# A selective-scan network: pairs of images with 128 channels on the partitions, changed to one image with 64 channels times two states and the other stages streamed beside the scans

## The chip, the cores and the metric

One core of one Trainium2 chip. The metric is the device time of one execution, in microseconds (us); the kernel before takes 12205 us. Engines: PE is TensorE (PEld its weight loads), DVE is VectorE, ACT is ScalarE, POOL is GpSimd, SP issues DMAs. PSUM is the memory that PE's products land in. The text takes each engine's instructions as carried out in their compiled order; in the changed kernel's trace VectorE's 7546 are.

## The reference, cut to what matters

Four images of 56x56 pixels and 96 channels pass four layers. Two of them hold a selective scan over 3136 positions, in four directions, with 192 channels and 16 states each:

```python
dt  = softplus(einsum(dt_raw, dtw) + dtb)          # dt_raw, b, c: projections of seq
d_a = exp(dt[..., None] * -exp(A_log))             # 192 x 16 per position
d_b = dt[..., None] * b[:, :, None, :]
def step(h, inp):
    da_t, db_t, x_t, c_t = inp
    h = da_t * h + db_t * x_t[..., None]           # the scan
    return h, einsum('bds,bs->bd', h, c_t)         # sum over the 16 states
y = ys + seq * D
# around it: layer norms, gates, 3x3 convolutions, a feed-forward;
# layers 2 and 3: linear attention and an fp8-quantized feed-forward
```

## The kernel before

A pair of images is loaded and passes all stages, one stage after the other. In the scan, 128 partitions hold 128 channels (a third tile holds the last 64 channels of both images). There are 3072 units (a chunk of 784 positions, a tile, a state). In each, ScalarE computes `da`; PE spreads the row of B over the partitions, into PSUM; VectorE multiplies it by `du` = dt times u and runs the scan; GpSimd multiplies the result `hs` by C, which gives `hc`; and PE adds `hc` up over the states:

```python
self.psum = ctx.enter_context(tc.tile_pool(name="psum", bufs=4, space=...PSUM))   # 4 tiles of 2 banks, for all uses
...
        yp = self.ps()                               # sums over the states of this slot
        def add_up(n, hc):
            for h in range(2):
                nc.tensor.matmul(yp[:, h, :HC], self.ident, hc[:, h * HC : (h + 1) * HC],
                                 start=n == 0, stop=n == NS - 1)
        ...
        for n in range(NS):
            ...
            nc.scalar.activation(da, dt, AF.Exp, scale=self.negA[l][:, t // 2, k, n : n + 1])
            db = b_of                                # PSUM: B spread over the partitions by PE
            nc.vector.tensor_tensor(db, du, db, ALU.mult)
            if n < NS - 1:
                b_of = spread_b(n + 1)
            if hc is not None:
                add_up(n - 1, hc)
            nc.vector.tensor_tensor_scan(hs[:, way], da[:, way], db[:, way], ..., ALU.mult, ALU.add)
            ...
            nc.gpsimd.tensor_tensor(hc, hs, cb, ALU.mult)    # times C
```

Of the four PSUM tiles one holds the sums, so three are free for spreads of B and the projections. (Cuts are marked by dots; the comments in code cuts are mine.)

## Time and profile before

| | before |
|---|---|
| time, median of its runs | 12205 us |
| four scans (windows of the prediction) | 9979 us |
| VectorE busy in a scan | 87% |
| all other stages | 2228 us |
| mean granted PE clock | 0.915 |

The prediction below shows and reads the lines. One line that it does not show matters later, the granted PE clock in 40 equal slices of the span, in tenths of full speed:

```profile
PEclk9999999899999989899989999998999999888999
```

### The profile page before, as it was taken

How to read it: one execution, taken by the hardware profiler on the slowest of the kernel's cores; microseconds unless marked ns; L12 is line 12 of the kernel's file. 1: busy time of each engine (PE TensorE's matmuls, PEld its weight loads, DVE VectorE, ACT ScalarE, POOL GpSimd, SP SyncE). 2: the span in 40 equal slices, each digit the busy share in tenths (PEclk: the TensorE clock that was granted, in tenths of full speed). 3: DMA queues.
4: the chain of work that ended last, by engine and by line, in shares of the span. 5: the costliest groups of instructions: out<-in, count | busy, mean ns of one | idle time of the engine just before them, and what ended most of it. 6: DMA issues, size and time to landing. Idle time of an engine off the chain costs nothing. (4 is left out here: it accounts for less than half of the span.)

```text
span 12206.9 us, 96092 instructions
## 1 busy us (share of the span) xinstructions
PE 9365.6 (77%) x32080; PEld 4295.8 (35%) x32080; DVE 9606.5 (79%) x7881; ACT 4411.3 (36%) x4763; POOL 6200.5 (51%) x5541
## 2 busy tenths in 40 slices
PE   6777777779777777779977777777787777777798
PEld 3333333334333333334533333333343333333345
DVE  6888888862888888893668888888638888888936
ACT  4333333332333333332343333333323333333323
POOL 3666566630666665660036666656316666656600
PEclk9999999899999989899989999998999999888999
DMA  4444434331444443440034443444214444333400
GB/s 126 125 128 126 122 120 127 119 93 49 128 126 128 124 122 120 122 124 24 4 122 127 128 126 121 122 122 124 88 55 127 126 128 125 119 120 120 124 24 9
DMA packets 279497, 1316.86 MB, mean 108 GB/s; under 512 B 61980, under 2 KB 72972, under 8 KB 278008
## 3 DMA queue, kind: packets, MB, share of 16 engines
q1 hardware_dynamic: 278080, 1307.13, 35.2%
q8 instruction: 252, 4.13, 0.1%
q10 hardware_dynamic: 920, 3.60, 0.1%
q14 instruction: 245, 2.01, 0.1%
HBM read 1270.44 MB, written 40.14 MB: 107 GB/s over the span
## 5 line engine op out<-in xcount | busy, mean ns | idle before, releaser
L552 PE MATMUL ps<-hc,ident 128*128 128x392 f32 x12288 | 5280.7, 560 | 2002.4 <-POOL hc L592 1998.1
L592 POOL TENSOR_TENSOR hc<-hs,X 128x784 f32<-128x784 f32 x3072 | 5667.8, 1850 | 864.6 <-DVE hs L586 522.7
L578 ACT ACTIVATE da<-dt,negA 128x784 f32<-128x784 f32 x3072 | 2913.0, 949 | 5786.7 <-DVE hs L586 5786.6
L586 DVE TENSOR_TENSOR_SCAN hs<-da,carry,ps 128x784 f32<-128x784 f32 x2304 | 4130.8, 1830 | 6.4
L552 PEld LDWEIGHTS ps<-hc,ident 128*128 128x128 f32 x12288 | 2316.0, 207 | 4579.2 <-POOL hc L592 3398.1
L580 DVE TENSOR_TENSOR ps<-du,ps 128x784 f32<-128x784 f32 x3072 | 2828.9, 963 | 560.2 <-PE ps L563 496.7
L590 POOL COPY carry<-hs 128x1 f32<-128x1 f32 x2304 | 474.9, 206 | 2240.8 <-DVE hs L586 2182.2
L586 DVE TENSOR_TENSOR_SCAN hs<-da,ps 128x784 f32<-128x784 f32 x768 | 1330.8, 1770 | 4.0 <-POOL hc L592 0.8
L501 POOL TENSOR_TENSOR bc<-rest,bc 32x784 bf16<-32x784 f32 x128 | 212.6, 1661 | 1871.0 <-ACT bc L500 1871.0
L560 PE MATMUL ps<-bc,sel 96*128 96x512 bf16 (+1 forms) x4096 | 936.2, 336 | 153.2 <-DVE hs L586 150.1
L563 PE MATMUL ps<-bc,sel 96*64 96x512 bf16 (+1 forms) x4096 | 546.8, 384 | 205.0 <-DVE hs L586 203.5
L560 PEld LDWEIGHTS <-sel 96*128 96x128 bf16 x4096 | 385.2, 99 | 819.5 <-issue 383.7
L532 DVE TENSOR_TENSOR du<-dt,U 128x784 f32<-128x784 f32 x192 | 345.7, 1800 | 364.3 <-ACT dt L527 364.3
L511 PE MATMUL ps<-dtr,dtw 12*128 12x392 f32 (+1 forms) x512 | 267.8, 654 | 238.4 <-ACT dtr L498 238.4
L563 PEld LDWEIGHTS <-sel 96*64 96x64 bf16 x4096 | 204.7, 121 | 668.5 <-DVE hs L586 316.8
L496 DVE TENSOR_TENSOR rest<-ps,bc 96x784 f32<-96x784 f32 x128 | 123.9, 968 | 390.9 <-ACT bc L495 373.3
L482 PE MATMUL ps<-U,w 128*108 128x392 f32 (+1 forms) x512 | 316.3, 704 | 0.0
L486 PE MATMUL ps<-U,w 128*108 128x392 f32 (+1 forms) x512 | 313.1, 697 | 0.0
L666 PE MATMUL ps<-Y,diag 128*128 128x392 f32 x864 | 289.0, 496 | 3.8 <-DVE diag L690 3.8
L527 ACT ACTIVATE dt<-ps,c 128x784 f32<-128x784 f32 x192 | 175.1, 914 | 233.4 <-PE ps L511 126.1
L511 PEld LDWEIGHTS ps<-dtr,dtw 12*128 12x128 f32 (+1 forms) x512 | 106.2, 229 | 369.1 <-ACT dtr L498 298.1
L361 PE MATMUL ps<-ln_r,spread 128*96 128x112 f32 x1792 | 212.9, 276 | 21.9 <-DVE ln_r L356 20.4
(177 smaller groups left out, 5459.8 us busy)
## 6 DMA issues: line engine op xcount, KB each, us to landing
X<-c SPq DMA_DIRECT2D x1024, 784.0 KB, 4.1
X<-c SPq DMA_DIRECT2D x1024, 392.0 KB, 5.2
z<-zs SPq DMA_DIRECT2D x48, 392.0 KB, 2.3
zl<-z SPq DMA_DIRECT2D x28, 672.0 KB, 4.5
x<-X SPq DMA_DIRECT2D x4, 2352.0 KB, 10.5
X<-x SPq DMA_DIRECT2D x4, 2352.0 KB, 13.7
c<-cf SPq DMA_DIRECT2D x128, 49.0 KB, 1.7
xin<-in_x_dram SPq DMA_DIRECT2D x4, 1176.0 KB, 8.8
```

The costliest lines, as they stand in the source:

```text
L482: nc.tensor.matmul(o, self.par("w128", f"{l}xw{k}a"), self.in_order(self.u3[:, j], orient, lo, HC), start=True, stop=False,)
L486: nc.tensor.matmul(o, self.par("w128", f"{l}xw{k}{j}"), self.in_order(self.u3[:, 2], orient, lo, HC), start=False, stop=True,)
L511: nc.tensor.matmul(ps[:, h, :HC], lhsT, rhs[t][:, h], start=True, stop=True)
L532: self.nc.vector.tensor_tensor(du.rearrange("p (a b) -> p a b", b=HS), dt.rearrange("p (a b) -> p a b", b=HS), self.in_order(self.u3[:, t] ...
L552: nc.tensor.matmul(yp[:, h, :HC], self.ident, hc[:, h * HC : (h + 1) * HC], start=n == 0, stop=n == NS - 1)
L560: nc.tensor.matmul(ps[:, s], self.sel[:, n, :], flat(bc[t])[:, s], start=True, stop=True)
L563: nc.tensor.matmul(ps[64 * j : 64 * j + 64, s], self.sel[:, n, :64], flat(bc[j])[:, s], start=True, stop=True,)
L578: nc.scalar.activation(da, dt, AF.Exp, scale=self.negA[l][:, t // 2, k, n : n + 1])
L580: nc.vector.tensor_tensor(db, du, db, ALU.mult)
L586: nc.vector.tensor_tensor_scan(hs[:, way], da[:, way], db[:, way], carry[:, t, n : n + 1] if step else 0.0, ALU.mult, ALU.add)
L590: nc.gpsimd.tensor_copy(carry[:, t, n : n + 1], hs[:, last : last + 1])
L592: nc.gpsimd.tensor_tensor(hc, hs, cb, ALU.mult)
```

## The change

Its intent: the scans are bound by VectorE and the other stages by PE, so let the stages of one image run while another image is scanned. One image at a time; 64 channels times two states on the partitions; what goes between stages passes through DRAM; the sums over states become pairs of products with 64 output columns; VectorE is relieved of some work. The diff has some 1700 lines; its core:

```diff
-        self.psum = ctx.enter_context(tc.tile_pool(name="psum", bufs=4, space=bass.MemoryType.PSUM))
+    def ps(self):                                   # everything else: 3 single banks
+        return self.psum.tile([128, 512], F32, tag="ps", name="ps", bufs=3)
+    def spread_b(self, ch, q):                      # B: 2 tiles of 2 banks
+        ps = self.psum.tile([128, 1024], F32, tag="b", name="b", bufs=2)
...
+        units = [(ch, g, q) for ch in chunks for g in range(NG) for q in range(NQ)]
...
+            nc.vector.tensor_tensor(db, ch.du[g], db, ALU.mult)
+            if n + 1 < len(units):
+                b = self.spread_b(units[n + 1][0], units[n + 1][2])
+            if late is not None:
+                self.add_up(*late)                  # sum of the unit before
+            nc.vector.tensor_tensor_scan(hs[:, way], da[:, way], db[:, way], ..., ALU.mult, ALU.add)
+            nc.scalar.copy(at, hs[:, end : end + 1])          # carry, was on GpSimd
+            nc.gpsimd.tensor_tensor(hc, hs, ch.cc[q // 2][:, q % 2], ALU.mult)
...
+        for h in range(2):                          # add_up: two states, 64 channels
+            nc.tensor.matmul(self.y[64 * h : 64 * h + 64, :HC], self.two,     # 128 x 64
+                             hc[:, h * HC : (h + 1) * HC], start=q == 0, stop=False)
...
+    for n, ch in enumerate(net.scans()):            # 8 phases: 2 layers x 4 images
+        ...
+            due = lengths[min(p, 7)] * u // (UNITS - NG * NQ)
+            while taken < due and next(rest, rest) is not rest:   # a step of another stage
+                taken += 1
+    for _ in net.tail(3):                           # the last image's tail, with nothing beside
+        pass
```

## The prediction

> **What bounds the kernel now.** I read the page's engine shares first, then the slices, then a table of windows cut where the scans begin and end, then the costliest groups, the waits of VectorE inside a scan, and one line by itself. (L... are lines of the kernel before.)
>
> ```profile
> PE 9365.6 (77%) x32080; PEld 4295.8 (35%) x32080; DVE 9606.5 (79%) x7881; ACT 4411.3 (36%) x4763; POOL 6200.5 (51%) x5541
> DVE  6888888862888888893668888888638888888936
> POOL 3666566630666665660036666656316666656600
> ```
>
> No engine is full over the span, but the slices show four long plateaus of VectorE at 8 or 9 tenths and between them holes where GpSimd falls to 0. The windows (columns: window, length, busy of PE, PEld, DVE, ACT, POOL, clock, DMA) give the sizes:
>
> ```profile
> 0.00:139.00 139.00, 90.18 (x482) 49.14 (x482) 55.41 (x89) 66.79 (x74) 8.30 (x20) 0.89 0.38 120
> 139.00:2641.00 2502.00, 1861.99 (x5594) 805.41 (x5594) 2184.85 (x1703) 920.31 (x988) 1542.43 (x1371) 0.91 0.41 124
> 2641.00:3027.00 386.00, 341.04 (x1334) 182.92 (x1333) 105.95 (x117) 111.67 (x118) 9.78 (x12) 0.95 0.12 39
> ...
> 5516.00:6234.00 718.00, 625.51 (x3514) 360.42 (x3512) 334.56 (x399) 252.51 (x286) 5.88 (x4) 0.93 0.10 29
> ...
> 11609.00:12207.00 598.00, 536.24 (x3033) 309.82 (x3032) 287.22 (x355) 189.70 (x220) 0.00 (x0) 0.95 0.05 13
> ```
>
> Four scans (two pairs of images, two layers) take 2502, 2489, 2499 and 2489 us, together 9979. The rest, 139 + 386 + 718 + 387 + 598 = 2228 us, is norms, convolutions, attention and feed-forward, bound by PE (536 of 598) while VectorE is under half busy. In a scan VectorE is busy 2185 of 2502 (87%), ScalarE 37%, GpSimd 62%. Which instructions these are:
>
> ```profile
> L592 POOL TENSOR_TENSOR hc<-hs,X 128x784 f32<-128x784 f32 x3072 | 5667.8, 1850 | 864.6 <-DVE hs L586 522.7
> L586 DVE TENSOR_TENSOR_SCAN hs<-da,carry,ps 128x784 f32<-128x784 f32 x2304 | 4130.8, 1830 | 6.4
> L580 DVE TENSOR_TENSOR ps<-du,ps 128x784 f32<-128x784 f32 x3072 | 2828.9, 963 | 560.2 <-PE ps L563 496.7
> L586 DVE TENSOR_TENSOR_SCAN hs<-da,ps 128x784 f32<-128x784 f32 x768 | 1330.8, 1770 | 4.0 <-POOL hc L592 0.8
> L532 DVE TENSOR_TENSOR du<-dt,U 128x784 f32<-128x784 f32 x192 | 345.7, 1800 | 364.3 <-ACT dt L527 364.3
> L602 DVE SCALAR_TENSOR_TENSOR Y<-ps,wts,Y 128x392 f32<-128x392 f32 x192 | 141.5, 781 | 46.2 <-PE ps L552 46.2
> L496 DVE TENSOR_TENSOR rest<-ps,bc 96x784 f32<-96x784 f32 x128 | 123.9, 968 | 390.9 <-ACT bc L495 373.3
> ```
>
> The 3072 pairs of a multiply and a scan cost 4130.8 + 1330.8 + 2828.9 = 8290.5 us of VectorE, with almost no idle before a scan. The idle of the scans, 4 x some 310 us, stands in front of du, rest and the first multiply behind them (364 + 391 + 560 us): the projections of the next chunk are made in VectorE's way, 64 times some 20 us.
>
> **What the Trainium skill says.** "SBUF — State Buffer", section "SBUF: two separate sides": a VectorE instruction with two SBUF inputs, or in a two-port mode, and a GpSimd instruction that reads SBUF exclude each other for a whole instruction. The trace agrees:
>
> ```profile
> L532 DVE TENSOR_TENSOR du<-dt,U x192: 949/1722/3003, 118.5 to 11533.6; 128x784 f32<-128x784 f32 x192
> L580 DVE TENSOR_TENSOR ps<-du,ps x3072: 944/964/989, 125.9 to 11594.8; 128x784 f32<-128x784 f32 x192
> ```
>
> The same size with one PSUM input never leaves 944 to 989 ns; with two SBUF inputs it goes from 949 to 3003. "ScalarE: Activation LUTs", section "What ACT_TABLE_LOAD costs": 1283 ns and a drain of 1380 ns. The loads of this trace take 1283 ns; in ScalarE's timeline the next instruction starts 0.01 us after one, so I see no drain and count 1283. "TensorEngine Tiling (Array Packing)", section "Available Configurations": an array of 128 rows by 64 columns is two tiles, which work independently. The trace has such pairs:
>
> ```profile
> L511 PE MATMUL ps<-dtr,dtw 12*128 12x392 f32 x256 | 135.1, 659 | 121.9 <-ACT dtr L498 121.9
> L514 PE MATMUL ps<-dtr,dtw 12*64 12x392 f32 x256 | 89.2, 845 | 0.0
> ```
>
> 128 columns occupy PE 135.1/256 = 0.53 us each, 64 columns 89.2/256 = 0.35, though one lasts longer: they overlap. (An fp32 matmul is two instructions in the trace.)
>
> **The change part by part.** *The scan core keeps its size.* The partitions hold 64 channels times two states in place of 128 channels, so 8 phases x 4 directions x 4 chunks x 3 groups x 8 state pairs = 3072 multiplies and scans of 128x784, as before, same operands: 8290 us. Nothing of that is gained.
>
> *VectorE loses* du (345.7, to GpSimd) and the sums into Y (141.5 + 130.0, now a matmul with the identity and a ScalarE copy). rest stays: 256 halves, some 133 us. *It gains beside the scans* what was in the holes. By my count of the compiled instructions at widths of 448: three loads, 21 x 0.62 = 13 us; four middles, six operations a chunk, 28 x 3.7 = 104; three tails, 21 x 13.2 = 277 (six in fusion, two in each gram, some eleven in each feed-forward). Together 394. Of these about 413 have two SBUF inputs or a fast fp16 form, and each can meet a GpSimd instruction of 1.85 us; from du (mean 1.80 against an undisturbed mean near 1.30) I put 0.7 us each: 290. Sum in the scans 8290 + 133 + 394 + 290 = 9107 us.
>
> *GpSimd:* hc 5668, du doubled (each half of the partitions needs it) 384 x 1.85 = 710, bc 213, small powers and memsets near 100; carry (475) leaves. 6700 us, not a bound by itself.
>
> *ScalarE:* da 2913; 2304 carries at an estimated 0.2 = 460; 768 softplus halves at 0.6 = 460; 768 copies of y at 0.5 = 385; projections' copies near 600; the rest of the net some 650; and 1051 table loads, where the page had some 140, because Exp alternates with Softplus, Silu and Gelu: 1051 x 1.283 = 1350. Sum 6800 us.
>
> *PE:* the sums over states become pairs of 64 columns, half of 5281 at best, so 2700 to 3500; spreading B near 1400; the other products 3500 to 4000. Some 8000. DMA falls: C is fetched once per chunk for all three groups, 1024 x 0.4 MB = 411 MB in place of most of 1307 MB.
>
> *Idle in the scans.* The next chunk is prepared a third of a chunk ahead, which should remove most of the 1240 us. But only two PSUM buffers are left for B, and on PE the spread for unit n+2 stands behind the sum of unit n-1, which waits for hc. The compiled order has 1141 places with two multiplies in a row. After scans ending at -1.8 and 0, hc ends at about 0.05, the sum near 0.9, the spread near 1.4, where the second multiply wanted it at 0.96: 0.45 us for perhaps half of them, 250 us. Each of 512 du and bc on GpSimd pushes hc by 1.7 to 1.85 us; say a third shows, 300. 224 chains of a norm (PE, ScalarE, power on GpSimd, PE, VectorE), beside the scans fewer, 0.5 each, 100; reloading U for 8 images, 60; other waits 100. These do not simply add, because a stall lets the others catch up; I take 650.
>
> *What is exposed.* Before the first scan: constants, folding, one image, near 130. After the last: the tail of one image. The tail of two took 598, bound by PE; one has less PE work (near 220 us by its matmuls) but only two chunks in flight and long chains: 340.
>
> Sum: 9107 + 650 + 130 + 340 = **10230 us** predicted, 16% under 12205.
>
> **The rivals.** *GpSimd and PE hold the scan through the buffers* (two of B, hs and hc each): if every insertion cost its full 1.85 us and every pair its 0.45, idle would be near 1450, some 11000 us. For it: everything runs in order, and hc ends just when it is wanted; against: GpSimd has 1 us spare in each unit. *ScalarE starves VectorE of da:* a table load out and back with a softplus is 3.2 us, gelu more, with da only three deep (5.6 us of scans). 6800 of 10000 speaks against a bound, bursts for it; 10600. *VectorE is simply full:* idle of 2%, shorter tail; 9107 + 180 + 450 gives 9740. *The stages beside do not fit* or their queues stall as the projections do today: 9979 for the scans as now, plus 394 + 290, less 617 moved away, plus 470, gives 10500. None reaches 12205; for that hiding would have to win nothing of 2228.
>
> **Range and chances.** From VectorE full (9740) to the buffers holding it in half of the cases (10700): 9750 to 10700. Faster by over 2% means under 11961: 0.96; within 2% 0.025; slower 0.015.
>
> **What would show it.** Right: multiplies and scans 3072 each near 960 and 1830 ns; VectorE at 91 to 95% in the scans; no holes in GpSimd's row until the end; tail(3) near 340 us; DMA bytes under half; sums on PE near 0.25 us busy per instruction. Wrong: multiplies that wait for PE in thousands of small gaps (buffers), scans that wait for ScalarE (tables), two-input operations far over 1.3 us, or a tail over 500 us. If GpSimd's hc grows beyond 1.85 us, the unit itself was misjudged.

## The result, and the profile after

The changed kernel takes 12851 us (median; 12819 to 12870 in 4 runs), against 12205 in the same rounds: ratio 1.052 (95% interval 1.050 to 1.055), **5% slower** where 16% faster was foretold. All ratios in this text are the mean time of one kernel's runs over that of the other's of the same rounds, so they are not quite the ratio of the medians quoted.

The first part of the page of the changed kernel, and two of its slices' rows:

```profile
PE 10724.2 (83%) x32510; PEld 3416.3 (27%) x32510; DVE 9010.8 (70%) x7546; ACT 6582.8 (51%) x10422; POOL 6985.7 (54%) x3964
DVE  4776777667776777767776666877668776777722
PEclk6766667766667667776767677766777667776665
```

The holes between the scans are gone, as intended, but VectorE is at 6 or 7 tenths where it was 8 or 9. And the row of the clock is the surprise: 6 and 7 tenths nearly everywhere, a mean of 0.689 in place of 0.915. Windows, cut at the first and the last scan (length, busy of PE, PEld, DVE, ACT, POOL, clock, DMA):

```profile
147.00:12274.00 12127.00, 10192.21 (x30858) 3118.33 (x30858) 8887.00 (x7246) 6441.77 (x10142) 6908.60 (x3865) 0.69 0.21 52
12274.00:12868.00 594.00, 442.34 (x1387) 246.75 (x1386) 102.12 (x221) 95.80 (x205) 50.84 (x57) 0.59 0.10 30
```

VectorE's 8887 us in the scans are close to the foretold 9107. Its idle there is 12127 - 8887 = 3240 us, and 650 were foretold. The costliest groups that answer to those of before (count, busy, mean ns, idle before and what ended most of it):

```profile
L537 POOL TENSOR_TENSOR hc<-hs,cc 128x784 f32<-128x784 f32 x3072 | 5704.9, 1870 | 4545.8 <-DVE hs L531 3550.0
L551 PE MATMUL y<-hc,two 128*64 128x392 f32 x12288 | 4120.3, 740 | 1294.4 <-POOL hc L537 1219.0
L524 DVE TENSOR_TENSOR b<-du,b 128x784 f32<-128x784 f32 x3072 | 2963.4, 970 | 2481.5 <-PE b L483 2468.6
L531 DVE TENSOR_TENSOR_SCAN hs<-da,carry,b 128x784 f32<-128x784 f32 x2304 | 4166.1, 1834 | 149.4 <-ACT da L522 91.7
```

The multiply and the scan take what they took (970 and 1834 ns), so does GpSimd's product. But in front of the multiply VectorE now waits 2469 us for PE's spread of B, in 1474 gaps. ScalarE, with its table loads, makes its scans wait only 113 us. The sums on PE (L551) occupy 4120/12288 = 0.335 us each, where the prediction hoped for 0.25 and half of the former 0.43 would be 0.215. How the clock shows in single instructions, from the timeline of the changed kernel (start, us, what):

```profile
3001.47 1.67 PE L455 MATMUL ps<-dtr,wd 12*128 12x392 f32 x2
...
3010.09 0.92 PE L455 MATMUL ps<-dtr,wd 12*128 12x392 f32 x2
```

The same two instructions take 1.67 us at one place and 0.92 at another; the clock's own records in the trace give 0.5 for the first place and 1.0 for the second. They know just these two values; the half lasts 8014 us in all in the changed kernel and 2083 in the one before. The two largest waits of PE (us in total, times, longest) are short ones:

```profile
PE y L551 <- POOL hc L537: 1219.0, 1240, 2.6
PE b L483 <- DVE hs L531: 486.3, 469, 3.7
```

Two counts that no view prints, made from the instructions in the traces, matter below. First, call a multiply that follows another multiply on VectorE, with no scan between, a *double*; the order is fixed when the kernel is compiled. The changed kernel has 1056 doubles (the prediction counted 1141). VectorE stands 1284 us in front of doubles and 1191 us in front of all other multiplies. Second, while VectorE stood there, 2475 us in all, PE was idle for only 40: it worked at spreads for 892 us, at sums for 552, at projections and the finishing of `y` for 503, and at other stages for 489. So VectorE waits for a PE that is busy with what stands in front of the spread.

### The profile page after: what moved, and what is told of

Same layout as the page of the kernel before. It is cut to its first block, busy times and chain, and to the rows that moved or that the text cites. A ratio compares the mean times of both kernels' runs of the same rounds, so it can differ in the third digit from the quotient of the medians. Undisturbed runs are those within 1.5% of the kernel's fastest.

```text
span 12868.3 us, 101763 instructions
## 1 busy us (share of the span) xinstructions
PE 10724.2 (83%) x32510; PEld 3416.3 (27%) x32510; DVE 9010.8 (70%) x7546; ACT 6582.8 (51%) x10422; POOL 6985.7 (54%) x3964
## 5 line engine op out<-in xcount | busy, mean ns | idle before, releaser
L537 POOL TENSOR_TENSOR hc<-hs,cc 128x784 f32<-128x784 f32 x3072 | 5704.9, 1870 | 4545.8 <-DVE hs L531 3550.0
L551 PE MATMUL y<-hc,two 128*64 128x392 f32 x12288 | 4120.3, 740 | 1294.4 <-POOL hc L537 1219.0
L524 DVE TENSOR_TENSOR b<-du,b 128x784 f32<-128x784 f32 x3072 | 2963.4, 970 | 2481.5 <-PE b L483 2468.6
L531 DVE TENSOR_TENSOR_SCAN hs<-da,carry,b 128x784 f32<-128x784 f32 x2304 | 4166.1, 1834 | 149.4 <-ACT da L522 91.7
L522 ACT ACTIVATE da<-dt,na 128x784 f32<-128x784 f32 x3072 | 2862.0, 945 | 728.9 <-DVE hs L531 714.1
L483 PE MATMUL b<-bc,sel 96*128 96x512 bf16 (+1 forms) x6144 | 2110.7, 436 | 489.9 <-DVE hs L531 486.3
L551 PEld LDWEIGHTS y<-hc,two 128*64 128x64 f32 x12288 | 839.8, 178 | 3117.3 <-POOL hc L537 2320.1
L531 DVE TENSOR_TENSOR_SCAN hs<-da,b 128x784 f32<-128x784 f32 x768 | 1346.3, 1774 | 54.4 <-ACT da L522 21.5
L431 PE MATMUL ps<-U,wd 64*108 64x392 f32 (+1 forms) x1536 | 864.0, 774 | 0.0
L461 POOL TENSOR_TENSOR du<-dt,U 128x784 f32<-128x784 f32 x384 | 783.0, 2047 | 147.0 <-ACT dt L456 138.9
L593 POOL TENSOR_TENSOR rs<-rs,power 112x4 f32<-112x4 f32 x252 | 257.4, 1021 | 964.6 <-ACT rs L592 784.8
L522 ACT ACT_TABLE_LOAD x511 | 655.6, 1283 | 8.3
L456 ACT ACT_TABLE_LOAD x339 | 434.9, 1283 | 78.9 <-PE ps L455 73.7
```

Source lines behind the costliest of these rows:

```text
L431: nc.tensor.matmul(ps[:m, :HC].rearrange("p (a b) -> p a b", b=HS), self.wx[rows, g, :m], self.in_order(self.U[rows, g], orient, c * CS + ...
L456: nc.scalar.activation(dt[:, h * HC : (h + 1) * HC], ps[:, :HC], AF.Softplus, bias=dtb[:, g : g + 1])
L461: nc.gpsimd.tensor_tensor(du.rearrange("p (a b) -> p a b", b=HS), ch.dt[g].rearrange("p (a b) -> p a b", b=HS), self.in_order(self.U[:, g] ...
L483: self.nc.tensor.matmul(ps[:, s], w, ch.bc[:, s], start=True, stop=True)
L522: nc.scalar.activation(da, ch.dt[g], AF.Exp, scale=ch.na[:, g, q : q + 1])
L524: nc.vector.tensor_tensor(db, ch.du[g], db, ALU.mult)
```

## The experiments

**Theory A (clock).** The paired 64-column sums use the array half as long; the granted clock then falls to a half for most of the time, each spread comes late, and VectorE waits for it. **Theory B (buffers and order).** With two tiles for B where the kernel before had three free, and the spread standing on PE behind a sum that waits for GpSimd, VectorE must wait whatever the clock. **Theory C.** The stages beside get in the way. Fifteen kernels ran. The five with the stages after the scans (sections 6 and 7) have a single run; I use them only for differences of some per cent between their phases. (A phase is the 384 units of one image and layer.)

### 1. Give PE its work back

```diff
+        nc.vector.tensor_scalar_mul(self.two, self.two, 0.5)
-        for h in range(2):
-            nc.tensor.matmul(..., self.two, hc[...], start=q == 0, stop=False)
+        for again in range(2):
+            for h in range(2):
+                nc.tensor.matmul(..., self.two, hc[...], start=q == 0 and again == 0, stop=False)
```

> The changed kernel with every sum over states issued twice at half weight (result unchanged), so PE has the array work per unit that the kernel before had. Theory A (the paired 64-column sums leave PE so idle that its clock is granted at half for 62% of the time, and the slow spread of B is what VectorE waits for): the clock rises from 0.689 to over 0.85, the first multiply's waits for the spread fall from 2469 us to under 1700, and the time falls below 12400 us although PE has more to do. Theory B (PE's order and two buffers of B, the clock being a by-product): more PE work in front of each spread makes the waits longer, over 3000 us, and the time over 13300 us.

12174 us, ratio to before 0.9975 (0.996 to 0.999): **5.3% less than the changed kernel by doing its sums twice.** The scans' window, the sums and VectorE's first wait in this run:

```profile
147.00:11581.00 11434.00, 10152.54 (x43136) 3587.33 (x43136) 8964.11 (x7245) 6399.95 (x10076) 6889.16 (x3864) 0.93 0.22 55
```

```profile
L553 PE MATMUL y<-hc,two 128*64 128x392 f32 x24576 | 5400.7, 542 | 997.3 <-POOL hc L538 911.0 <-issue 71.4 <-POOL du L462 1.0
```

```profile
DVE b L525 <- PE b L484: 1586.2, 957, 11.4
```

PE is busy for the same 10150 us with some 12,280 more matmul instructions: the clock is 0.93 in the scans in place of 0.69, and a matmul of the sums occupies PE 5401/24576 = 0.220 us in place of 0.335. The waits fall from 2469 to 1586 us. Theory A's numbers came in, all three; theory B's direction did not. But the compiler also ordered the instructions anew around the added ones: this kernel has 469 doubles in place of 1056. The wait in front of doubles fell from 1284 to 158 us, and that in front of all other multiplies rose from 1191 to 1436. So this run alone cannot part the clock from the order; section 4 has a step where the number of doubles hardly changes. And 1586 us of waits stay, and the kernel is still no better than the one before: the clock is not the whole of it.

### 2. The paired sums put into the kernel before

```diff
-                    yp[:, h, :HC], self.ident, hc[:, h * HC : (h + 1) * HC], ...
+                    yp[64 * h : 64 * h + 64, 0, :HC], self.ident[:, :64], hc[:, h * HC : (h + 1) * HC], ...
```

> The kernel before with its sums over states as pairs of 64 columns, as the changed kernel has them (wrong result on purpose: only a part of the channels is summed; same shapes otherwise). Theory A: the granted clock in the scans falls from 0.91 to about 0.7, because the array is used half as long; the time grows by 2 to 6% if PE then holds the scan up even with three free buffers for B, or stays within 2% if they hide it. If the clock stays over 0.88, the pairs are not what lowers it.

The first scan's window in this kernel:

```profile
139.00:2659.00 2520.00, 1777.85 (x5591) 451.81 (x5592) 2191.51 (x1703) 919.42 (x987) 1526.04 (x1371) 0.66 0.41 123
```

The clock in the scan is 0.66 in place of 0.91, from this one edit. So the paired sums do lower it. The time is 12311 us, ratio 1.008 (1.007 to 1.010): the kernel before hardly minds. Its 1410 doubles (1468 without the edit) cost VectorE 7 us of waiting in all, at the low clock. (The result is wrong on purpose; the comparison's tolerance let it pass all the same.)

### 3. Take away the third buffer, with and without the pairs

In the kernel before, four PSUM tiles less one for the sums leave three; with three tiles two are left, as many as the changed kernel has for B.

```diff
-        self.psum = ctx.enter_context(tc.tile_pool(name="psum", bufs=4, space=bass.MemoryType.PSUM))
+        self.psum = ctx.enter_context(tc.tile_pool(name="psum", bufs=3, space=bass.MemoryType.PSUM))
```

> The kernel before with three PSUM tiles in place of four: one for the sums and two for B and all else, as the changed kernel has for B. Clock high, wide sums. If two buffers alone are the loss: over 3% slower than before. If they cost only together with the low clock: within 2%, scans of 2490 to 2550 us each in place of 2490.

> The same with the paired sums too (wrong result on purpose, as in the run of paired sums). If clock and buffers act together: the scans lose much more than the two alone (0.8% for the pairs), 5% or more, 2700 us or more for each scan, with the multiply waiting for the spread. If they only add: below 3.5% in all.

| kernel before with | clock | four scans, first to last | time | ratio |
|---|---|---|---|---|
| four tiles, wide sums | 0.915 | 9972 us | 12205 | 1 |
| four tiles, paired sums | 0.711 | 10062 | 12311 | 1.008 |
| three tiles, wide sums | 0.892 | 10842 | 13102 | 1.074 |
| three tiles, paired sums | 0.664 | 11973 | 14234 | 1.166 |

The group of the multiply with three tiles, wide sums, then the same with paired sums:

```profile
L580 DVE TENSOR_TENSOR ps<-du,ps 128x784 f32<-128x784 f32 x3072 | 2943.3, 965 | 1049.3 <-PE ps L563 715.5 <-PE ps L560 315.4 <-ACT dt L527 7.1
```

```profile
L581 DVE TENSOR_TENSOR ps<-du,ps 128x784 f32<-128x784 f32 x3072 | 2961.4, 967 | 2222.3 <-PE ps L561 1136.8 <-PE ps L564 1073.5
```

VectorE's idle in front of the multiply goes from 560 us to 1049 without the third buffer and to 2222 with the low clock as well. The two causes do not add: in the scans the paired sums cost 90 us with three buffers free and 1131 us with two. Of the first expectation the branch "over 3%" came in (7.4%), so two buffers are a loss at a high clock too; of the second the branch "much more", with 2991 to 2996 us a scan. Here a slow spread is harmless while a third one is ready. Not all of the 1131 us need be the clock: the last kernel was also compiled with more doubles, 1312 in place of 752. In front of them VectorE waits 1671 us in place of 174, which is 1.27 us each in place of 0.23, so their number alone does not make it. (The tiles also serve the projections and the other stages, so 870 us is the price of the tile, not of B's buffer alone. Outside the scans the time hardly moved: 2254 us against 2235, span less the four scans.)

### 4. The sums one unit later, and doses of added work

To take the sum that waits for GpSimd out of the spread's way, the sum of unit n-2 follows the spread of unit n+1 (with a third buffer of `hc`, and one of the weights `wd` for room):

```diff
-            if late is not None:
-                self.add_up(*late)
+            if len(late) == 2:
+                self.add_up(*late.pop(0))
```

> The changed kernel with the sum of unit n-2 in place of n-1 put behind the spread of unit n+1 (three buffers of hc, one of the direction's weights to make room), so that PE does not stand waiting for GpSimd in front of a spread. Theory B: VectorE's waits for the spread fall from 2469 to under 1500 us and the time to 11500 to 12000 us at a clock near 0.69. Theory A: the spreads stay slow at the low clock, waits over 2000 us, time over 12500 us.

12629 us, ratio 1.035, clock 0.761; the waits for the spread are 2375 us. So 1.7% off, theory B's 11500 to 12000 missed, and theory A's numbers came in: at a low clock, order alone is a small part. (The clock rose too, from 0.689, so even the 1.7% need not be the order's.) Then with sums twice, and with only every second unit's sum twice (`for again in range(1 + q % 2)`):

> The sums twice and one unit later, overlapped. The later sums alone took 1.7% off at a low clock. At the full clock, theory B expects the waits for the spread to fall from 1586 to under 1100 us and the time from 12174 to 11600 to 11900 us; if PE's order in front of the spread is not the cause, it stays within 1% of 12174.

> The sums later, and only every second unit's sum twice. Clock between 0.761 (single) and 0.908 (twice), some 0.84; time between 12629 and 11969 us, some 12250, if the time follows the clock. If PE was too full with all sums twice, below 11969.

| sums later, and | clock | waits for the spread | doubles, wait before them | time | ratio |
|---|---|---|---|---|---|
| once | 0.761 | 2375 us | 1210, 1166 us | 12629 | 1.035 |
| every second one twice | 0.868 | 1833 | 1159, 867 | 12150 | 0.995 |
| all twice | 0.908 | 1378 | 614, 274 | 11969 | 0.981 |

The time follows the clock dose by dose, though PE has more to do each time. From the first row to the second the number of doubles is nearly the same, so fewer doubles do not explain these 479 us; this is the cleanest evidence for the clock. From the second to the third the doubles are halved as well. The expectation for half doses came in; that for all twice, 11600 to 11900 us with waits under 1100, was too good. The last, at 11969 us, **has a lower time than both kernels**: by 1.95% (interval 1.8 to 2.1) than the one before, which is at the 2% from which the record calls a kernel faster, so that its verdict is "unclear".

### 5. Added work right in front of the wait

```diff
-        for s in (slice(0, 512), slice(512, CS)):
-            self.nc.tensor.matmul(ps[:, s], w, ch.bc[:, s], start=True, stop=True)
+        for _ in range(2):
+            for s in (slice(0, 512), slice(512, CS)):
+                self.nc.tensor.matmul(ps[:, s], w, ch.bc[:, s], start=True, stop=True)
```

> The changed kernel with only the spread of B issued twice (the second writes the same values over the first). This puts the extra PE work directly in front of the multiply that waits for it, 0.33 us more on that path for each unit at the full clock. Theory A (clock): the clock still rises, to over 0.8, and the time falls below 12700 us. Theory B (only what stands in front of the spread counts): each unit waits longer and the time rises over 13000 us.

12869 us, ratio 1.054, against the changed kernel's 1.052: no difference shown; clock 0.771, waits 2317 us. Both expectations missed. The clock rose by 0.08, and added work of another kind raises it too. That what it gave was spent by twice the spread is the likely reading, not shown: this kernel has 622 doubles, another order again. So it seems to be no free choice where the added work goes.

### 6. The stages after the scans

In each of the eight phases the stages run when its units are nearly through, not beside them:

```diff
-        if u >= 1:
-            due = lengths[min(p, 7)] * u // (UNITS - NG * NQ)
-            if u >= UNITS - NG * NQ:
-                due = 10**6
+        if u == UNITS - NG * NQ:
+            due = 10**6
```

> The changed kernel with the other stages after each phase's scans in place of beside them. It tells how long 384 units of scan take with nothing beside. Theory A: the clock stays low, since the scan alone has even less for PE, and a phase takes 1350 to 1500 us where VectorE's own work is 1036 + 17; 8 phases 10800 to 12000, and with some 2000 us of stages 13000 to 14000 in all. Theory C (the stages beside get in the way of the scans: queues and two-input operations): the phases alone take 1080 to 1150 us each, 9000 in all.

> The stages after the scans and the sums twice: the scan core at the full clock with two buffers of B. A phase took 1384 to 1456 us at a clock near 0.55 with single sums. Theory A alone (only the clock): 1080 to 1150 us a phase. Theory A and B (buffers and order of PE keep a share): 1200 to 1330 us.

| stages after | a phase (384 units) | eight phases | clock | whole |
|---|---|---|---|---|
| sums once | 1384 to 1456 us | 11320 us | 0.621 | 14456 |
| sums twice | 1229 to 1326 us | 10218 us | 0.878 | 13240 |

The phases of the first kernel came in at theory A's 1350 to 1500 us (its whole time is above the 13000 to 14000 foretold), those of the second at "theory A and B". (The clock in the first one's phases was 0.60 to 0.62, not near 0.55 as the expectation has it. The second also has fewer doubles, 566 in place of 1140, so its 1100 us are not the clock's alone.) The scans with nothing beside take 11320 of the 12127 us that they take overlapped. So the stages beside add only some 800 us, of which some 450 are VectorE's work and the rest is waiting. In the serial kernel 14456 - 11320 = 3136 us lie outside the phases; some 740 of them, the start and the last tail, are exposed in either kernel, so overlap hides near 2400 us at a price of 800: it works, and theory C falls as the main cause. It is the core that is slow: 10218 us even at the high clock, against 8290 + 133 of VectorE's own work.

### 7. A third buffer, a second bank for the sums: no gain

The changed kernel lays out eight banks of PSUM, as the one before did: three for all else, four for B, one for `y`. Three buffers of B leave one bank for all else (`ps` bufs 3 to 1, `b` bufs 2 to 3, spread two units ahead); its control has two of B and one bank. In all of these one product of a stage takes a tile of B's as well.

> As the run before, with three PSUM buffers of B and the spread issued two units ahead; the other products share one PSUM bank in place of three, which the serial order bears. Theory B: a phase falls to 1060 to 1120 us, the 1036 us of VectorE's multiplies and scans and little more. If the phase stays over 1200 us, what holds the core is not the number of buffers but the projections or the GpSimd product.

> The control of the run with three buffers of B after the scans: two buffers of B and one bank for all else, sums twice, stages after. With three buffers a phase took 1281 to 1306 us. If the third buffer helps: this one takes over 1350 us. If it does not: 1260 to 1310.

> The changed kernel, overlapped, with the sums twice, three buffers of B, the spread two units ahead and one bank for all else. If B's buffers are the rest of the loss: 11000 to 11700 us and waits for the spread under 800 us. If the one bank now holds back the stages and the projections, which is the price: no better than the 12174 us of the sums twice alone.

With the stages after, the eight phases sum to some 10350 us (three buffers) and 10255 (the control), without the hole of 308 to 323 us that a stage cuts into each of the last three: with a single bank for all else the third buffer gives nothing, and theory B's 1060 to 1120 us a phase missed. VectorE then waits 625 us for the spread in place of 1328, but 1186 us for GpSimd's product, which itself waits 1927 us for sums on PE (857 in the control). Overlapped, it is 14033 us, ratio 1.149: the single bank is far too little, as the second branch of its expectation has it. So the third buffer could not be tried in the changed kernel with all else equal.

Last, two banks for the sums and two for all else (`y` bufs 1 to 2, `ps` bufs 3 to 2), on top of twice and later:

> The sums twice and later (11969 us), with two PSUM banks for the sums of a group and two in place of three for all else. In the idle by place in a chunk, the places just after a change of group stand out; if that is the wait of the next group's first sum for ScalarE to copy the last group's y, idle there falls and the time is 11500 to 11850 us. If the missing third bank costs the stages beside as much, it stays within 1%.

> The same with the stages after the scans: the scan core alone. With sums twice and one y bank a phase took 1229 to 1326 us. If order and y bank are the rest of the core's loss: 1080 to 1150 us a phase, near VectorE's 1053. If it stays over 1200, the projections of the next chunk are what remains.

12068 us, ratio 0.988, against 0.981 without: a little slower. Alone the phases take 1243 to 1332 us, not 1080 to 1150. Both expectations of a gain missed. So either the hand-over of `y` is not what holds the core, or the third bank, which all else lost, was worth as much; these runs do not part the two.

## Why the prediction was wrong, point by point

**Right.** 3072 multiplies and scans of 970 and 1834 (1774) ns; VectorE's busy time in the scans (8887 us, foretold 9107); GpSimd 6986 (6700); ScalarE 6583 (6800), and its table loads hidden; no holes in GpSimd's row before the end; DMA bytes half of before (662.6 of 1316.9 MB, so just not under). Near by luck: the stages beside cost the scans 807 us where 684 were foretold as VectorE's work and contention, but that work was only some 450 (VectorE's busy time in the scans, 8883 against 8433 in the serial kernel). And the spread of `du` from 949 to 3003 ns, read as contention with GpSimd, is in part the order of reading: the 64 of 192 that overlapped no GpSimd instruction took some 975 or some 1612 ns, the 128 others 2054 on average. Of the prediction's own signs of being wrong two came: multiplies that wait for PE in 1474 gaps, and a tail of 594 us.

**The step that failed: idle in the scans, 650 us foretold, 3240 measured.** The path was among those it named: VectorE's multiply waits for PE's spread of B behind other work of PE. But one term was mis-sized, two things were left out, and they were added up the wrong way.

*Left out: the PE clock.* The prediction worked with PE times of the kernel before, at its clock of 0.91, and said of the sums "half of 5281 at best, so 2700 to 3500". They took 4120, because the clock fell to 0.69; at 0.93, with the sums twice, they did take half, 0.220 us each in place of 0.43. The edit in the kernel before shows that the paired sums lower the clock (0.91 to 0.66 in the scan), and the doses of added work show that the time falls as the clock rises. What the clock costs the changed kernel is not measured alone. The sums twice gave back 693 us in the scans (12127 to 11434), and 1100 us where the scans run alone (single runs), both with fewer doubles as well; from the later sums once to the half dose the whole time fell by 479 us with nearly as many doubles.

*Mis-sized: the pair of multiplies that waits for its spread, "0.45 us for perhaps half of them, 250 us".* In front of doubles VectorE waited 1284 us, 1.2 us for each of the 1056. At the clock that I had assumed the term would have been about right: 158 us for 469 doubles with the sums twice.

*Left out: multiplies that follow a scan or a stage's instruction.* For them the prediction had no term of its own; the nearest are its 300 us for GpSimd pushing `hc` and "other waits 100". VectorE waited 1191 us in front of them, and 1436 at the high clock. I had reckoned one spread behind one sum; PE's order holds projections and stages too, and they are 992 of the 2435 us that PE worked while VectorE stood.

*The clock and the buffers together.* With three tiles free the paired sums cost the kernel before 90 us, with two 1131; one tile less alone costs 870 us in its scans, at a high clock. The prediction summed its idle terms and noted that they add up to less than their sum; here they added up to more. That this interaction is what turned a gain into a loss in the changed kernel is likely from the same pattern of waits, not shown by an experiment in it.

*Mis-sized beside the idle: what is exposed, 130 + 340 foretold, 147 + 594 measured.* The window of the tail shows PE busy 442 us at a clock of 0.59, where I had near 220 us of PE work at full clock; no run tried a deeper pipeline there. This is 271 us of the whole miss; the idle is 2590.

**The rivals.** "GpSimd and PE hold the scan through the buffers" was the right name, at 11000 us, but worked out at the clock of the kernel before. ScalarE's bursts did not matter. Nothing in my list reached 12205: the list had no rival in which an engine gets slower by being relieved.

**Open.** Of the core's idle at the high clock (10218 against 8423 us), a second bank for `y` gave no gain while all else had two banks, nor did a third buffer of B while all else had one; the later sums took off 1.7% once and twice, in both cases with another compiled order. No experiment held the compiled order fixed. How the rest parts among projections, two buffers of B and three banks for all else is not settled, since all eight banks were in use and none could be given to one of them alone.

## What to carry to other kernels

Before counting on a PE saving, look at the granted clock and at who waits for PE: in a kernel where PE is not the bound, less array work gave a lower clock, and every short product on another engine's path became slower. Count buffers and clock together: here a third PSUM buffer hid a clock of 0.66 almost wholly, two did not hide even a clock of 0.89. And when an engine is found waiting for PE at a low clock, one cheap test is to issue some matmul twice at half weight: if the time falls, the clock is a suspect. Then compare the order of the instructions in the two traces, since here the compiler changed it with every such edit, and try a dose between.

## What the Trainium skill lacked or had wrong

- "TensorE: Matmul & The Clock Gate", section "HAM oscillation — how this bites in real kernels", gives "no PE-idle gaps >~3.4µs" as the rule, and the page has the clock half or full while one core is busy, which the two values in these traces confirm. Taken alone the rule is not enough: in the scans of the changed kernel PE showed 5 gaps over 3.4 us in 12127 us (8 in one scan of the kernel before, 2500 us long) and was busy 84%, yet the clock was at a half for 61% of the time. The page's next section also blames frequent short idles, without a limit; but PE was idle less here (16%) than in a scan of the kernel before (26%), at a lower clock. There, pairs of 64-column products in place of 128-column ones lowered the clock from 0.91 to 0.66 with PE busy 71% in place of 74% (and 32 gaps over 3.4 us in the scan); in the changed kernel the same pairs issued twice raised it from 0.69 to 0.93. The page does not say how paired tiles count as activity.
- "TensorEngine Tiling (Array Packing)", section "Performance Considerations", names a fixed overhead of each matmul and PSUM evacuation as what can limit the gain, not the clock: here the pairs took 5% off PE's busy time in a scan of the kernel before (1862 to 1778 us), where half of its sums would have been some 35% (they are 1320 of the 1862 us). At the clock of 0.93 the sums did take half, 0.220 us in place of 0.43.
- "ScalarE: Activation LUTs", section "What ACT_TABLE_LOAD costs", has 1283 ns and a drain of some 1380 ns. The loads here take 1283 ns; no drain shows: the next instruction starts 0.01 us later, and before 511 of the loads ScalarE was idle for 8.3 us in all.
- No page that I read has a time for a power on GpSimd: on 112x4 elements it took 1021 ns, 252 times, 257 us in all, where I had allowed near 100 for these and all memsets.
